# A residual adapter with layer norm: block turns read contiguously, and another plan of who does what

## Chip, cores and metric

One core of a Trainium2 chip runs the whole program. The metric is device time in microseconds of one launch; lower is better.

## The reference, cut to what matters

x holds 128 batches of 128 rows and 512 columns, in fp32. Each batch b has a language number, which picks its W1 (512×128), b1, W2 (128×512), b2, gamma and beta out of ten.

```python
h = relu(einsum('bsh,bha->bsa', x, W1[ids]) + b1[ids][:, None, :])
adapted = einsum('bsa,bah->bsh', h, W2[ids]) + b2[ids][:, None, :]
y = x + adapted
normed = (y - mean(y)) * rsqrt(var(y) + 1e-5)          # along the 512 columns
out = x + normed * gamma[ids][:, None, :] + beta[ids][:, None, :]
```

## The kernel before, in words

One batch is one tile: 128 rows on the partitions, 512 columns. x is loaded four batches at a time (`load_x`, L80) and stored two at a time (`store`, L464). W2 and the spread rows of b2, gamma and beta stay in SBUF, as does W1 of all ten languages once it is loaded (from batch 17 on).

The path of a batch b, engine by engine:

- TensorE transposes the four 128-column blocks of x into PSUM (`transpose_x`, L317), ScalarE copies them to SBUF (`copy_xT`, L325). ScalarE copies the batch's W1 into its own tile (`stage_w1`, L311), since the language number is known at run time only. TensorE multiplies W1 by the transposed x, four accumulated products into PSUM (`down`, L342); ScalarE adds b1 and applies relu (`relu`, L352); TensorE multiplies by W2 into one of five PSUM buffers (`up`, L356).
- GpSimd adds x and b2 beforehand (`add_b2`, L329, into one of four buffers) and x and beta into the output tile (`add_beta`, L335). VectorE adds the former to the product, with the sum of each row as a by-product (`residual`, L380); ScalarE takes the sum of squares (`square`, L403) and, for two batches at once, the mean and the first guess of the reciprocal root; VectorE refines that in three small steps (`rstd`), then applies mean and gamma (`scale`, L448) and the reciprocal deviation and beta (`finish`, L457). `finish` frees the PSUM buffer and completes the output.

Three letters vary the path, in patterns of 16 batches:

- `KINDS`, between batch `MIDDLE` and batch 128 - `LAST`: an "E" batch is *seeded*. ScalarE copies x into the PSUM buffer first (`seed`, L307), the product accumulates onto it, and VectorE's `residual` adds b2 by the register of the batch's language. GpSimd then adds only beta. A "P" batch has x + b2 from GpSimd. Outside, the kind is "-": there GpSimd adds b2 too, or, for a few batches, VectorE in an instruction of its own (`vector_b2`, L375).
- `TURNS`, from batch `TURNED` on: a "T" batch goes as above. A "w" batch has its W1 loaded from HBM by a DMA of SyncE (`load_late`, L572) instead of ScalarE's copy. An "F" batch is *turned*: its W1 is loaded from HBM (`load_first`, L169), its x is loaded a second time, block by block, so that 32×32 blocks lie where they belong (`load_blocks`, L284, four DMAs of 64 KB), and VectorE transposes all of these blocks in one instruction (`turn_blocks`, L291). Neither TensorE's transposes nor ScalarE's copy are needed for it.

W1 tiles and the second copies of x share seven buffers (`wp`).

The order of the work is written out by a plan. Each step is entered with a due time in units of batches (`at`, `at_pair`, L641 to L694); the steps are issued in the order of these times, and `keep` (L57) holds each engine to that order. `BATCH` has the times of the steps of one batch relative to its number, `PAIR` those of two batches 2g and 2g+1 relative to 2g + 3; `EDGE` takes the place of `PAIR` where one of the pair's kinds is "-". The engines wait for each other by semaphores alone. `lid` (L151) loads four language numbers into an engine's registers; it stands in that engine's queue like any other step. Batches 123 to 127 and the end are written out by hand (L699 to L849).

Of the kernel before, what the change touches and what calls it, by code (L numbers as in the profile page):

```python
# [8 lines left out]
FP = mybir.dt.float32  # L9
# [4 lines left out]
ET = mybir.EngineType  # L14
PSUM = bass.MemoryType.PSUM

P = 128
G = 4
# [2 lines left out]
EARLY = 17  # L21
LATE = 17
U = 2
MIDDLE = 27
TURNED = 31
LAST = 8
KINDS = 'EPPPPPEPEEPPEPPP'
TURNS = 'TTTTFTTTTTwwFTTw'
SEEDED = 'E'
ON_GPSIMD = 'P'  # L30
BATCH = dict(turn=-0.49, copy=0.12, r=0.1, beta=-0.56, relu=1.24, w1=-0.83, up=2.11, load=-5.63, r_late=-0.51)
SEED = {'E': 1.88}
PAIR = dict(stat=0.23, square=0.35, means=1.55, root=1.82, scale0=2.66, n1=2.4, n2=3.195, n3=3.37, scale1=3.4, end0=3.66, end1=4.28)
EDGE = dict(stat=0.59, square=0.73, means=1.74, root=2.0, scale0=3.04, n1=2.83, n2=3.375, n3=3.69, scale1=4.03, end0=4.06, end1=4.58)


@with_exitstack
def cond_resid_kernel(ctx: ExitStack, tc: tile.TileContext, x, itok, W1, b1, W2, b2, gamma, beta, out):
# [8 lines left out]
    nc = tc.nc  # L47
    B, S, H = x.shape
    L, _, A = W1.shape
    KC = H // P  # L50
# [6 lines left out]
    def keep(ins):  # L57

        engine = ins.ins.engine
        if engine in last:  # L60
            tc.add_manual_dep(ins.ins, last[engine], behind, reason="kept order")
        last[engine] = ins.ins.name
        return ins
# [6 lines left out]
    wp = ctx.enter_context(tc.tile_pool(name="wp", bufs=7))  # L70
# [7 lines left out]
    E = B - 5  # L78
# [11 lines left out]
    rows = rp.tile([P, H], FP, tag="r", name="rows")  # L90
    b1r = const.tile([L, A], FP, name="b1r")
    w1 = const.tile([P, L, KC, A], FP, name="w1")
# [49 lines left out]
    lids, w1s = {}, {}  # L142
# [8 lines left out]
    def lid(b, engine):  # L151
        g = b // G
        if (g, engine) not in lids:
            loads, vals = nc.values_load_multi_w_load_instructions(
                lang[0:1, g * G : (g + 1) * G],
                engines=[engine],
                min_val=0,
                max_val=L - 1,
                skip_runtime_bounds_check_because="clamped on the chip to 0..L-1 above",
            )  # L160
            for ins in loads:
                keep(ins)
            lids[g, engine] = vals
        return lids[g, engine][b % G]
# [102 lines left out]
    def kind(b):  # L267
        return KINDS[b % len(KINDS)] if MIDDLE <= b < B - LAST else "-"

    def turn(b):  # L270
        return TURNS[b % len(TURNS)] if TURNED <= b < B - LAST - 2 else "-"

    def seeded(b):
        return kind(b) in SEEDED
# [7 lines left out]
    x2s = {}  # L282

    def load_blocks(b):  # L284
        x2s[b] = wp.tile([P, H], FP, tag="w1s", name=f"x2_{b}")
        for i in range(KC):
            src = x[b, :, i * P : (i + 1) * P].rearrange("(j c) e -> c j e", c=32)
            dst = x2s[b][32 * i : 32 * (i + 1), :].rearrange("c (j e) -> c j e", j=4)
            keep(nc.sync.dma_start(out=dst, in_=src))

    def turn_blocks(b):  # L291
        xT[b] = tp.tile([P, H], FP, tag="xT", name=f"xT_{b}")
        src = x2s.pop(b).rearrange("p (j r k) -> p j k r", j=4, k=KC)
        dst = xT[b].rearrange("p (j k c) -> p j k c", j=4, k=KC)
        keep(nc.vector.transpose(dst, src))

# [170 lines left out]
    def on(b):  # L467
        return 0 <= b < B
# [172 lines left out]
    def at(when, step, *args):  # L641
        plan.append((when, len(plan), step, args))

    for b in range(B):
        if b >= 20 and b % G == 0:
            at((11 if b == 20 else b - 7) - 0.01, load_x, b // G)
        if b >= 3:
            for n, engine in ((b + 5, ET.Activation), (b + 5, ET.PE), (b + 2, ET.DVE), (b + 6, ET.Pool)):
                if on(n):
                    at(b + 0.99, lid, n, engine)  # L650
        if turn(b) in "Fw":
            at(b + BATCH["load"] - 1, lid, b, ET.SP)
            at(b + BATCH["load"], load_first if turn(b) == "F" else load_late, b)
        if turn(b) == "F":
            at(b + BATCH["load"], load_blocks, b)
            at(b + BATCH["turn"], turn_blocks, b)
        elif 5 <= b <= E - 2:
            at(b, transpose_x, b)
            at(b + BATCH["copy"], copy_xT, b)
        if 4 <= b <= E - 3:  # L660
            add_to = b + (BATCH["r"] if seeded(b) else BATCH["r_late"])
            at(add_to, add_b2, b)
            at(b + BATCH["beta"], add_beta, b)
            at(b + 1.1, down, b)
            at(b + BATCH["relu"], relu, b)
        if seeded(b):
            at(b + SEED[kind(b)], seed, b)
        if FIRST <= b <= E - 1 and turn(b) not in "Fw":
            at(b + BATCH["w1"], stage_w1, b)
        if 2 <= b <= E - 4:  # L670
            at(b + BATCH["up"], up, b)

    begun = [(step, n) for n in (E - 7, E - 6, E - 5) for step in (vector_b2, residual, square)]
    begun += [(scalar_means, E // 2 - 3), (deviation, E // 2 - 3), (scale, E - 7), (rstd, E // 2 - 3, 1)]
# [1 line left out]
    def at_pair(g, when, step, *args):  # L676
        if g < E // 2 - 3 or (step, *args) in begun:
            at(2 * g + 3 + when, step, *args)

    for g in range(E // 2 - 1):  # L680
        b = 2 * g
        when = EDGE if "-" in (kind(b), kind(b + 2)) else PAIR
        for j in (0, 1):
            at_pair(g, j + when["stat"] - 0.01, vector_b2, b + j)
            at_pair(g, j + when["stat"], residual, b + j)
            at_pair(g, j + when["square"], square, b + j)
        at_pair(g, when["means"], scalar_means, g)
        at_pair(g, when["root"], deviation, g)
        for n in (1, 2, 3):
            at_pair(g, when[f"n{n}"], rstd, g, n)  # L690
        for j in (0, 1):
            at_pair(g, when[f"scale{j}"], scale, b + j)
            at_pair(g, when[f"end{j}"], finish, b + j)
        at_pair(g, when["end1"] + 0.001, store, g)  # L694
# [192 lines left out]
```

## Time and profile before

| | |
|---|---|
| median of 3 runs | 303.43 us (302.5 to 304.01) |
| profiled execution | 303.28 us, its span 301.5 us |
| granted TensorE clock, mean | 0.996 |
| moved by DMA | 88.1 MB, 292 GB/s on average |

The profile is of one execution. A row of a group gives the line, the engine, the operation, the tiles that it writes and reads, the count, the busy time, and the mean duration of one in ns. PE is TensorE, PEld its weight loads, DVE VectorE, ACT ScalarE, POOL GpSimd, SP SyncE. An instruction of an engine usually begins some 0.1 us before the one ahead of it is recorded as ended, so a step from start to start is shorter than a duration. A row of the waits says who waited for whom, for how long in all, how often, and the longest.

### The profile page before, as it was taken

To read this page: it belongs to the slowest core of one execution; us is meant where nothing else is said; L and a number is where in the kernel's file an instruction comes from. 1 tells how busy PE (TensorE), PEld (TensorE's weight loads), DVE (VectorE), ACT (ScalarE), POOL (GpSimd) and SP (SyncE) were. 2 spreads that over 40 slices of the span, in tenths; PEclk is the share of its full clock that TensorE was granted. 3 is DMA by queue.
4 is the path that set the end of the run, shared out by engine and by line. 5 is a ranking of instruction groups with operands and counts; after the bars stand their busy time and mean duration, and the time that the engine had idled before them with its cause. 6 is when DMAs were issued, how large, how long until landed. Compare 5 with 4: busy or idle time off the path is not lost.

```text
span 301.5 us, 7148 instructions
## 1 busy us (share of the span) xinstructions
PE 294.0 (98%) x1783; PEld 216.9 (72%) x1783; DVE 291.9 (97%) x775; ACT 273.1 (91%) x760; POOL 272.8 (90%) x229
## 2 busy tenths in 40 slices
PE   7999999999999999999999999999999999999993
PEld 3858787767777777777777777777677777777761
DVE  5999999999999999999999999999999999999995
ACT  4978789889999989999999989999999999999883
POOL 1199998999999999999999999999998999989852
PEclk9999999999999999999999999999999999999998
DMA  6999999987869899799997999699997899884625
GB/s 227 390 388 365 346 331 400 405 307 227 318 237 315 245 365 282 252 312 321 315 299 241 305 312 308 253 314 293 330 292 229 269 296 363 287 279 150 224 79 215
DMA packets 61724, 88.10 MB, mean 292 GB/s; under 512 B 3274, under 2 KB 24277, under 8 KB 61683
## 3 DMA queue, kind: packets, MB, share of 16 engines
q1 hardware_dynamic: 61622, 87.59, 86.7%
q8 instruction: 15, 0.25, 0.3%
q14 instruction: 27, 0.21, 0.2%
q10 hardware_dynamic: 60, 0.05, 0.1%
HBM read 54.07 MB, written 33.55 MB: 291 GB/s over the span
## 4 chain that ended last, share of the span: by engine, by line
PE 55%; DVE 21%; issue 11%; DMA 6%; ACT 4%; DVEq 1%; SPq 1%; POOL 0%; ACTq 0%; POOLq 0%
PE ph L346 21%; PE py L368 18%; PE pxT L323 10%; DVE py L452 6%; DVE py L386 6%; PE py L360 5%; DVE o L461 5%; DMA w<-in_L_cond_W_dram 3%; DMA out_dram<-o 2%; ACT sq L409 1%; DMA w1s<-in_L_cond_W_dram 1%; DVE o L546 1%; ACT xT L327 1%; DVE py L378 1%; DVE part L425 1%
## 5 line engine op out<-in xcount | busy, mean ns | idle before, releaser
L340 POOL TENSOR_TENSOR o<-x,beta_b 128x512 f32<-128x512 f32 x121 | 153.3, 1282 | 14.0 <-DVE beta_b L258 12.7
L346 PE MATMUL ph<-xT,w1s 128*128 128x128 f32 x1024 | 135.4, 275 | 0.0
L346 PEld LDWEIGHTS ph<-xT,w1s 128*128 128x128 f32 x1024 | 125.7, 192 | 6.9 <-ACT hT L354 5.7
L333 POOL TENSOR_TENSOR r<-x,b_b 128x512 f32<-128x512 f32 x85 | 108.8, 1280 | 3.6 <-DVE rstd L428 3.6
L368 PE MATMUL py<-w,hT 128*128 x200 | 104.0, 601 | 0.9 <-DVE o L461 0.6
L323 PEld LDWEIGHTS pxT<-ident,x 128*128 128x128 f32 x468 | 60.9, 150 | 59.9 <-issue 39.3
L452 DVE SCALAR_TENSOR_TENSOR py<-py,nmean,gamma_b 128x512 f32<-128x512 f32 x124 | 92.8, 749 | 1.7 <-issue 1.7
L409 ACT ACTIVATE sq<-py,sum 128x512 f32<-128x512 f32 x124 | 85.8, 692 | 7.9 <-DVE rstd L428 5.8
L461 DVE SCALAR_TENSOR_TENSOR o<-py,rstd,o 128x512 f32<-128x512 f32 x116 | 85.5, 747 | 0.0
L327 ACT COPY xT<-pxT 128x512 f32<-128x512 f32 x117 | 68.5, 585 | 5.5 <-PE pxT L323 4.7
L323 PE MATMUL pxT<-ident,x 128*128 128x128 f32 x468 | 71.9, 277 | 0.0
L386 DVE SCALAR_TENSOR_TENSOR py<-py,r 128x512 f32<-128x512 f32 x90 | 62.2, 691 | 0.0
L354 ACT ACTIVATE hT<-ph,b1T 128x128 f32<-128x128 f32 x128 | 47.7, 373 | 5.9 <-PE ph L346 4.3
L314 ACT COPY w1s<-w 128x512 f32 x81 | 50.4, 622 | 0.0
L368 PEld LDWEIGHTS py<-w,hT 128*128 128x128 f32 x200 | 30.4, 191 | 4.9 <-DVE o L461 3.4
L360 PE MATMUL py<-w,hT 128*128 x56 | 29.3, 604 | 0.0
L409 ACT ACTIVATION_READ_ACCUMULATOR sq<-py,sum 128x1 f32 x124 | 25.8, 208 | 0.0
L386 DVE SCALAR_TENSOR_TENSOR py<-py,b_b 128x512 f32<-128x512 f32 x28 | 19.4, 692 | 0.4 <-PE py L360 0.2
L309 ACT COPY py<-x 128x512 f32<-128x512 f32 x28 | 16.7, 596 | 0.0
L419 ACT ACTIVATE root<-ssq,eps 128x2 f32<-128x2 f32 x62 | 16.5, 265 | 0.0
L400 ACT ACTIVATE nmean<-sum 128x2 f32<-128x2 f32 x61 | 12.9, 212 | 0.0
L386 DVE DVE_READ_ACCUMULATOR py<-py,r 128x1 f32 x90 | 12.6, 140 | 0.0
(79 smaller groups left out, 147.2 us busy)
## 6 DMA issues: line engine op xcount, KB each, us to landing
out_dram<-o SPq DMA_DIRECT2D x62, 512.0 KB, 5.0
x<-in_x_dram SPq DMA_DIRECT2D x27, 1024.0 KB, 7.2
w1s<-in_L_cond_W_dram SPq DMA_DIRECT2D x47, 256.0 KB, 6.3
x<-in_x_dram SPq DMA_DIRECT2D x10, 512.0 KB, 6.1
x<-in_x_dram SPq DMA_DIRECT2D x44, 64.0 KB, 4.0
w<-in_L_cond_W_dram SPq DMA_DIRECT2D x4, 640.0 KB, 8.2
w<-in_L_cond_W_dram SPq DMA_DIRECT2D x1, 1792.0 KB, 9.9
w<-in_L_cond_W_dram SPq DMA_DIRECT2D x1, 768.0 KB, 5.4
```

What stands on the lines that cost most here:

```text
L314: keep(nc.scalar.copy(w1s[b].rearrange("p k a -> p (k a)"), src))
L323: keep(nc.tensor.transpose(pxs[b][:, k, :], cols, ident))
L327: keep(nc.scalar.copy(xT[b], pxs.pop(b)))
L333: keep(nc.gpsimd.tensor_tensor(rs[b], xb(b), b2_b[:, bass.ds(v * H, H)], ALU.add))
L340: keep(nc.gpsimd.tensor_tensor(os[g][:, j, :], xb(b), beta_b[:, bass.ds(v * H, H)], ALU.add))
L346: nc.tensor.matmul(phs[b], lhsT=w1s[b][:, k, :], rhs=xT_of(b, k), start=(k == 0), stop=(k == KC - 1))
L354: keep(nc.scalar.activation(hT[b], phs.pop(b), AF.Relu, bias=b1T[:, bass.ds(lid(b, ET.Activation), 1)]))
L368: keep(nc.tensor.matmul(ys[b], lhsT=hT[b], rhs=w2[:, bass.ds(v * H, H)], start=not m, stop=True))
L386: nc.vector.scalar_tensor_tensor(ys[b], ys[b], 1.0, r, ALU.mult, ALU.add, accum_out=sum_of(b))
L409: nc.scalar.activation(sq, ys[b], AF.Square, bias=col(sums, b), scale=-float(H), accum_out=col(ssqs, b))
L452: nc.vector.scalar_tensor_tensor(ys[b], ys[b], col(nmeans, b), gamma_b[:, bass.ds(v * H, H)], ALU.add, ALU.mult)
L461: nc.vector.scalar_tensor_tensor(o, ys[b], rstds[g][:, j : j + 1], o, ALU.mult, ALU.add)
```

## The change

- `turn_blocks` reads its source so that the 32 columns of a block are neighbours. Before, they were four elements apart, and the columns of the transposed x were interleaved accordingly. The rows of W1 must be in the same order, so turned batches load W1 with the new `load_rows`: four DMAs of 32 partitions, each partition holding four rows that are 32 apart.
- `KINDS` has four E among 16 letters instead of five (place 9 is now P), between batches 26 and 123 instead of 27 and 119. `TURNS` has one w (place 9) instead of three (places 10, 11, 15); the two F, places 4 and 12, stay. Turned or late batches begin at 32 instead of 31 and end at 121 instead of 117.
- Batches of kind "-" take their steps' times from the new `BATCH_EDGE`, and all tables of times have new values.
- VectorE's `lid` is entered behind a `finish`, for the four batches that follow; before, it was entered at the end of the step of every fourth batch, for the batches from two further on.

```diff
-MIDDLE = 27
-TURNED = 31
-LAST = 8
-KINDS = 'EPPPPPEPEEPPEPPP'
-TURNS = 'TTTTFTTTTTwwFTTw'
+MIDDLE = 26
+TURNED = 32
+LAST = 4
+KINDS = 'EPPPPPEPEPPPEPPP'
+TURNS = 'TTTTFTTTTwTTFTTT'
-BATCH = dict(turn=-0.49, copy=0.12, r=0.1, beta=-0.56, relu=1.24, w1=-0.83, up=2.11, load=-5.63, r_late=-0.51)
-SEED = {'E': 1.88}
-PAIR = dict(stat=0.23, square=0.35, means=1.55, root=1.82, scale0=2.66, n1=2.4, n2=3.195, n3=3.37, scale1=3.4, end0=3.66, end1=4.28)
-EDGE = dict(stat=0.59, square=0.73, means=1.74, root=2.0, scale0=3.04, n1=2.83, n2=3.375, n3=3.69, scale1=4.03, end0=4.06, end1=4.58)
+BATCH = dict(turn=0.19, copy=0.16, r=-0.36, beta=-0.13, relu=1.26, w1=-0.77, up=2.66, load=-5.59, r_late=0.22)
+BATCH_EDGE = dict(copy=0.2, r=0.05, r_late=1.05, beta=1.06, relu=1.3, w1=-0.6, up=2.5)
+SEED = {'E': 1.69}
+PAIR = dict(stat=0.22, square=0.34, means=1.98, root=1.9, scale0=3.03, n1=2.43, n2=3.115, n3=3.28, scale1=3.4, end0=3.67, end1=4.32)
+EDGE = dict(stat=0.6, square=0.68, means=1.75, root=1.77, scale0=2.64, n1=2.65, n2=3.592, n3=3.62, scale1=3.64, end0=3.66, end1=4.66)
...
+    def load_rows(b):
+        w1s[b] = wp.tile([P, KC, A], FP, tag="w1s", name=f"w1s_{b}")
+        rows = W1[bass.ds(lid(b, ET.SP), 1)].rearrange("o (i k r) a -> i (o r) k a", i=4, k=KC)
+        for i in range(4):
+            keep(nc.sync.dma_start(out=w1s[b][32 * i : 32 * (i + 1)], in_=rows[i]))
+
     def turn_blocks(b):
         xT[b] = tp.tile([P, H], FP, tag="xT", name=f"xT_{b}")
-        src = x2s.pop(b).rearrange("p (j r k) -> p j k r", j=4, k=KC)
+        src = x2s.pop(b).rearrange("p (j k r) -> p j k r", j=4, k=KC)
         dst = xT[b].rearrange("p (j k c) -> p j k c", j=4, k=KC)
         keep(nc.vector.transpose(dst, src))
...
     for b in range(B):
+        when = BATCH_EDGE if kind(b) == "-" else BATCH
...
-            for n, engine in ((b + 5, ET.Activation), (b + 5, ET.PE), (b + 2, ET.DVE), (b + 6, ET.Pool)):
+            for n, engine in ((b + 5, ET.Activation), (b + 5, ET.PE), (b + 6, ET.Pool)):
...
-            at(b + BATCH["load"], load_first if turn(b) == "F" else load_late, b)
+            at(b + BATCH["load"], load_rows if turn(b) == "F" else load_late, b)
...
+        if b % G == 0 and on(b + G):
+            at_pair(g, when["end0"] + 0.001, lid, b + G, ET.DVE)
```

In the loop over the batches, the times of `copy_xT`, `add_b2`, `add_beta`, `relu`, `stage_w1` and `up` are read from `when` instead of `BATCH`. Counted over the program, ScalarE has 91 copies of W1 instead of 81 and 24 seeds instead of 28; GpSimd has 94 additions of b2 instead of 90; SyncE issues 44 + 17 + 9 loads of single W1 instead of 28 + 19; TensorE's instructions are the same ones.

More of the change, by code (lines that the diff above doesn't have):

```diff
@@ L658, in cond_resid_kernel @@
             at(b, transpose_x, b)
-            at(b + BATCH["copy"], copy_xT, b)
+            at(b + when["copy"], copy_xT, b)
         if 4 <= b <= E - 3:
-            add_to = b + (BATCH["r"] if seeded(b) else BATCH["r_late"])
-            at(add_to, add_b2, b)
-            at(b + BATCH["beta"], add_beta, b)
+            at(b + (when["r"] if seeded(b) else when["r_late"]), add_b2, b)
+            at(b + when["beta"], add_beta, b)
             at(b + 1.1, down, b)
-            at(b + BATCH["relu"], relu, b)
+            at(b + when["relu"], relu, b)
         if seeded(b):
@@ L668, in cond_resid_kernel @@
         if FIRST <= b <= E - 1 and turn(b) not in "Fw":
-            at(b + BATCH["w1"], stage_w1, b)
+            at(b + when["w1"], stage_w1, b)
         if 2 <= b <= E - 4:
-            at(b + BATCH["up"], up, b)
+            at(b + when["up"], up, b)
     begun = [(step, n) for n in (E - 7, E - 6, E - 5) for step in (vector_b2, residual, square)]
```

## The prediction

> **What bounds the kernel now.** I read the page first, for the load of each engine.
>
> ```profile
> span 301.5 us, 7148 instructions
> PE 294.0 (98%) x1783; PEld 216.9 (72%) x1783; DVE 291.9 (97%) x775; ACT 273.1 (91%) x760; POOL 272.8 (90%) x229
> PE 55%; DVE 21%; issue 11%; DMA 6%; ACT 4%; DVEq 1%; SPq 1%; POOL 0%; ACTq 0%; POOLq 0%
> ```
>
> Four engines are loaded to 90% or more, and the chain that ended last (third line) changes hands between TensorE and VectorE. Which of them sets the pace? The table of windows answers that for the middle, from the first weights of batch 36 to those of batch 116: 80 batches, that is five rounds of the 16-letter patterns, with ten block turns, 25 seeds and 15 late W1 loads.
>
> ```profile
> core 0: us, PE busy (x) PEld busy (x) DVE busy (x) ACT busy (x) POOL busy (x), PEclk, DMA share, GB/s
> 91.93:266.28 174.35, 173.91 (x1083) 130.29 (x1081) 174.00 (x451) 166.22 (x471) 170.72 (x140) 1.00 0.90 295
> 94.37:105.32 10.95, 10.95 (x72) 8.32 (x71) 10.92 (x30) 10.84 (x33) 10.95 (x10) 1.00 0.91 284
> ```
>
> VectorE is idle for 0.35 of 174.35 us: it is full. GpSimd is idle for 3.63, ScalarE for 8.13. TensorE looks full too, but its ends are modelled, so I go by its starts. TensorE's timeline, the rows of the down products only:
>
> ```profile
> 55.77 1.16 PE L346 MATMUL ph<-xT,w1s 128*128 128x128 f32 x8
> 58.38 1.06 PE L346 MATMUL ph<-xT,w1s 128*128 128x128 f32 x8
> 60.58 1.06 PE L346 MATMUL ph<-xT,w1s 128*128 128x128 f32 x8
> 63.23 1.06 PE L346 MATMUL ph<-xT,w1s 128*128 128x128 f32 x8
> 65.42 1.06 PE L346 MATMUL ph<-xT,w1s 128*128 128x128 f32 x8
> 68.04 1.06 PE L346 MATMUL ph<-xT,w1s 128*128 128x128 f32 x8
> ...
> 87.98 1.06 PE L346 MATMUL ph<-xT,w1s 128*128 128x128 f32 x8
> 89.74 1.05 PE L346 MATMUL ph<-xT,w1s 128*128 128x128 f32 x8
> 91.93 1.06 PE L346 MATMUL ph<-xT,w1s 128*128 128x128 f32 x8
> 94.37 1.06 PE L346 MATMUL ph<-xT,w1s 128*128 128x128 f32 x8
> ...
> 266.28 1.06 PE L346 MATMUL ph<-xT,w1s 128*128 128x128 f32 x8
> ```
>
> Undisturbed, a batch takes 2.19 us (89.74 to 91.93, or 63.23 to 65.42), and 1.76 where the next batch is turned by VectorE and its four TensorE transposes are left out (87.98 to 89.74). Right after a turn comes a stall: 91.93 to 94.37 is 2.44. By starts, TensorE needs 70 × 2.19 + 10 × 1.76 = 170.9 us for the middle and takes 174.35: **3.5 us of stall** in ten turns. Batches 21, 23 and 25 (the first six rows) stall by 0.42, 0.46 and 0.43: **1.3 us** more. The eleventh turn lies behind the window; at the mean of the ten it adds 0.35. So some **5.2 us** of TensorE's time is waiting, and no more can be won here without less work on TensorE. The table of waits says for what:
>
> ```profile
> PEld py L368 <- DVE o L461: 3.4, 14, 0.4
> DVE py L452 <- issue: 1.7, 4, 0.7
> POOL r L333 <- DVE rstd L428: 3.6, 3, 1.4
> POOL o L340 <- DMA out_dram<-o: 1.3, 1, 1.3
> POOL r L485 <- DVE py L386: 1.1, 1, 1.1
> ```
>
> An up product waits for a PSUM buffer that `finish` (L461) frees: TensorE stands because VectorE is late. VectorE's own idle time (second row) is four waits with no releaser, at a `scale` behind a load of batch numbers into registers (`lid`).
>
> **The change part by part.** *The turns.* Eleven before and eleven after (places 4 and 12, batches 36 to 116). Each reads with a step of 16 bytes now and contiguously then. The groups:
>
> ```profile
> L295 DVE STREAM_TRANSPOSE xT<-x 128x512 f32<-128x512 f32 x11 | 12.4, 1125 | 0.0
> L258 DVE STREAM_SHUFFLE beta_b<-four 128x512 f32<-128x512 f32 x10 | 6.6, 752 | 0.0
> L378 DVE TENSOR_TENSOR py<-py,b_b 128x512 f32<-128x512 f32 x6 | 4.2, 694 | 0.2 <-PE py L368 0.2
> ```
>
> The trace has no contiguous turn. Its bounds: 1125 ns, if the step costs nothing, and 694, the cheapest 512-column row here; reading fewer lines can't make it slower. I take 752, the shuffle, which also moves whole 512-column rows between partitions and reads contiguously: 373 ns less each, **4.1 us** in eleven (between 0 and 4.7). In the middle VectorE's load falls from 174.0 to 170.3, which is TensorE's 170.9: the pace passes to TensorE.
>
> A rule speaks against this gain: "VectorE: DVE Perf Modes" of the Trainium skill, section "The three transpose paths", gives 311 ns for a VectorE transpose of 128×128 in bf16. Four times that, an estimate, is 1244, which would make 1125 the normal price of 512 columns, and by it this term of the sum is nothing (rival A). "SBUF — State Buffer" of the Trainium skill, section "Door 1: The DMA port swizzle", speaks for the gain: SBUF is read in lines of 16 bytes and each new line costs, so a step of 16 bytes pays at every element. No run here shows yet which of the two holds.
>
> *The turn's place.* It moves behind `scale` of batch b-6 and a small step. Before, the turn of 36 ran from 89.09 and its product began at 91.93 on TensorE:
>
> ```profile
> 89.09 1.12 DVE L295 STREAM_TRANSPOSE xT<-x 128x512 f32<-128x512 f32 x1
> 90.12 0.72 DVE L452 SCALAR_TENSOR_TENSOR py<-py,nmean,gamma_b 128x512 f32<-128x512 f32 x1
> 90.75 0.16 DVE L425 SCALAR_TENSOR_TENSOR part<-part,root 128x2 f32<-128x2 f32 x1
> 90.82 0.70 DVE L386 SCALAR_TENSOR_TENSOR py<-py,r 128x512 f32<-128x512 f32 x1
> ```
>
> It ended at 90.21, 1.72 us early. The two steps take 0.70 (90.12 to 90.82) and the quicker turn gives 0.37 back, so 1.39 us of cover is left: nothing. Without the cover, TensorE would wait at each product of a turned batch.
>
> *W1 of these batches* now comes in four DMAs of 64 KB instead of one of 256 KB, in the same pieces and shape as the block loads of x:
>
> ```profile
> w1s<-in_L_cond_W_dram SPq DMA_DIRECT2D x47, 256.0 KB, 6.3
> x<-in_x_dram SPq DMA_DIRECT2D x44, 64.0 KB, 4.0
> L289 SPq DMA_DIRECT2D x<-in_x_dram x44: 312/430/1242, 76.8 to 255.0; - x44
> ```
>
> Three more issues of 0.43 us are 1.3 us on SyncE per turn; behind them queue the block loads of x, then stores and later loads. The loads start 5.6 batches ahead, 12 us at 2.19; eight issues and a landing are 8 × 0.43 + 4.0 = 7.4. Hidden. Ten late W1 loads fewer (16 to 6) take 2.6 MB of 88 off the queues.
>
> *Late loads and seeds.* Those ten W1 are copied by ScalarE again, and four seeds fewer are copied (24 for 28):
>
> ```profile
> 92.68 0.58 ACT L327 COPY xT<-pxT 128x512 f32<-128x512 f32 x1
> 93.16 0.62 ACT L314 COPY w1s<-w 128x512 f32 x1
> 93.67 0.37 ACT L354 ACTIVATE hT<-ph,b1T 128x128 f32<-128x128 f32 x1
> ```
>
> ```profile
> L309 ACT COPY py<-x 128x512 f32<-128x512 f32 x28 | 16.7, 596 | 0.0
> ```
>
> Such a copy holds the queue for 0.51 us (93.16 to 93.67), the seed, 26 ns shorter, about as long: 10 × 0.51 - 4 × 0.51 = 3.1 us more, in the middle 10 - 5 copies, 166.2 to 168.8. That fits under 170.9, barely.
>
> *GpSimd* gets the b2 addition of the batches no longer seeded (place 9, five batches; batch 120 becomes seeded): 94 for 90. An addition takes 170.72 / 140 = 1.22 us: **4.9 us more on an engine that has little left**. In the middle alone it needs 170.7 + 5 × 1.22 = 176.8, so it must live on its lead. How large is that? Before the sum for batch 123 it waited 4.9 us because it was ahead (3.6 + 1.3 in the table of waits), and that sum (GpSimd's timeline, then VectorE's) lay ready for a while:
>
> ```profile
> 280.83 1.28 POOL L485 TENSOR_TENSOR r<-x,b_b 128x512 f32<-128x512 f32 x1
> ```
>
> ```profile
> 286.15 0.69 DVE L386 SCALAR_TENSOR_TENSOR py<-py,r 128x512 f32<-128x512 f32 x1
> ```
>
> It ended at 282.11 and was used at 286.15: 4.04. So 4.9 + 4.0 - 4.9 = **4.0 us** is all that the rest may come earlier before GpSimd is late. The 1.3 in it, the wait for a store, should go: up to batch 25 the b2 addition now stands before the beta addition, so GpSimd reaches that beta one addition later.
>
> *Batches up to 25.* VectorE's two `finish` of a pair stood next to each other; now a residual, a `scale` and a small step lie between, so buffers come free evenly, and `lid` stands behind a `finish`, which covers it, instead of before a `scale`. I take the three stalls, 1.3 us, as gone (between 0 and 1.7, VectorE's four waits). The tail's pairs take the step times of the middle; its hand-written end is the same: nothing.
>
> *The sum.* VectorE could give 4.1 + 1.7 = 5.8, TensorE 5.2, GpSimd 4.0. The least counts: 4.0. As three engines then lie within 2% of each other in the middle (170.9, 170.3, 168.8) and the fourth has no spare, I take 0.5 off for waits that pass between them, about what VectorE, the bound, lost in the middle (0.35). The profiled execution took 303.28 us (its span of 301.5 and 1.8 around it): 303.28 - 3.5 = 299.8, and against the median of the runs, 0.15 higher, **299.9 us**.
>
> **The rivals.** *A: the turn is no quicker* (its time is the transposition's, not the step's; the change then does not do what it says). For: the trace shows no contiguous turn. Against: 1125 stands far above every other 512-column row. VectorE stays full in the middle, and only the early 1.3 is won: 303.28 - 1.3 = 302.0.
>
> *B: GpSimd binds harder.* The wait for the store stays (its landing is the queue's matter, not GpSimd's): 2.7 is then its allowance, less 0.5: 303.28 - 2.2 = 301.1.
>
> *C: slower, by ScalarE.* Its load would be 168.8 in a middle of 170.9, so 2.1 us of its 8.1 us of waiting may stay. If all of it stays, the middle takes 168.8 + 8.1 = 176.9, 2.6 more than before, and over the 98 batches of the patterns 3.2: 306.5; it turns slower from 5.5 us on. For: relu and square each wait for another engine. Against: in batches 37 to 41, with three seeds in five (second row of the windows), ScalarE was busy for 10.84 of 10.95 and TensorE kept 2.19 all the same.
>
> **How the numbers follow.** The forecast 0.58, A 0.17, B 0.13, C 0.12. The forecast's own range is 298.4 to 301.2. The range of 8 in 10 takes in B and A: 298.2 to 303.2; C is left out. A measurement of this kernel can tell 0.5%, 1.5 us. Faster by more (under 301.9): the forecast, most of B and a third of A, 0.72; within: the rest of A and B and a mild C, 0.18; slower: 0.10.
>
> **What would show it.** The turn's group near 750 ns instead of 1125; TensorE's step after a turn near 2.19 instead of 2.44; starts 2.19 apart from batch 20 to 26; GpSimd without its three waits for VectorE and, late, VectorE's residual waiting for GpSimd; ScalarE's waits in the middle near 2 us. A turn over 1.0 us, or new waits of TensorE for ScalarE, would make it wrong.

## The result, and the profile after

The changed kernel takes 300.69 us (median of ten runs, 300.02 to 301.93); the kernel before takes 303.69 beside it. The ratio is 0.9904, with an interval of 0.9881 to 0.9927: about 1% faster. One of the ten runs of the kernel before took 508.05 us; the ratio is of the others. The profiled execution took 301.23 us with a span of 298.8, where the one before had 303.28 and 301.5.

The head of the page, the load of each engine, and the shares of the chain that ended last, for the changed kernel:

```profile
span 298.8 us, 7251 instructions
PE 290.7 (97%) x1783; PEld 214.7 (72%) x1783; DVE 288.9 (97%) x775; ACT 277.2 (93%) x766; POOL 277.4 (93%) x233
PE 81%; DVE 6%; ACT 4%; DMA 3%; issue 3%; SPq 1%; DVEq 0%; POOL 0%; ACTq 0%; POOLq 0%
```

VectorE's share of the last chain fell from 21% to 6% and TensorE's rose from 55% to 81%: the pace has passed to TensorE. But TensorE still waits, and the groups and the windows show where. First the groups of the turn and of ScalarE's copies of W1 and of seeds:

```profile
L302 DVE STREAM_TRANSPOSE xT<-x 128x512 f32<-128x512 f32 x11 | 7.7, 703 | 0.0
L321 ACT COPY w1s<-w 128x512 f32 x91 | 56.7, 623 | 0.0
L316 ACT COPY py<-x 128x512 f32<-128x512 f32 x24 | 14.4, 599 | 0.0
```

A turn takes 703 ns instead of 1125. Now the windows of the changed kernel, with the columns of the prediction's table (span, then busy time of PE, PEld, DVE, ACT, POOL). The first row is the middle, batches 36 to 116; the second is the stretch from batch 36 to batch 44, the third that from 44 to 52, so both run from a turned batch to the next:

```profile
90.91:264.02 173.11, 173.11 (x1083) 129.35 (x1081) 171.00 (x451) 170.12 (x476) 173.11 (x141) 1.00 0.87 282
90.91:107.99 17.08, 17.08 (x110) 12.89 (x109) 16.98 (x46) 16.74 (x48) 17.08 (x14) 1.00 0.84 263
107.99:125.50 17.51, 17.51 (x111) 12.97 (x110) 17.24 (x46) 17.31 (x50) 17.51 (x16) 1.00 0.90 300
```

The middle takes 173.11 us, 1.24 less than before, but 2.2 more than the 170.9 that TensorE needs. The first stretch is exactly TensorE's need (7 × 2.19 + 1.75 = 17.08; 1.75 is the step ahead of a turned batch). The second is 0.43 longer, and ScalarE is busy in it for 17.31 us, more than TensorE's 17.08. The four later stretches of the second kind take 17.69, 17.50, 17.49 and 17.50, those of the first kind 17.08 or 17.09: the 2.2 us lie in the second kind alone. TensorE's timeline, the rows of the down products only, shows the places:

```profile
58.18 1.06 PE L353 MATMUL ph<-xT,w1s 128*128 128x128 f32 x8
...
69.15 1.06 PE L353 MATMUL ph<-xT,w1s 128*128 128x128 f32 x8
...
90.91 1.06 PE L353 MATMUL ph<-xT,w1s 128*128 128x128 f32 x8
93.10 1.06 PE L353 MATMUL ph<-xT,w1s 128*128 128x128 f32 x8
...
112.39 1.06 PE L353 MATMUL ph<-xT,w1s 128*128 128x128 f32 x8
114.64 1.16 PE L353 MATMUL ph<-xT,w1s 128*128 128x128 f32 x8
116.93 1.06 PE L353 MATMUL ph<-xT,w1s 128*128 128x128 f32 x8
119.12 1.06 PE L353 MATMUL ph<-xT,w1s 128*128 128x128 f32 x8
121.47 1.06 PE L353 MATMUL ph<-xT,w1s 128*128 128x128 f32 x8
```

The first two rows are batches 21 and 26: five steps in 10.97 us, 2.19 each; the early stalls are gone. Behind the turned batch 36 the step is 2.19 as well (90.91 to 93.10; before 2.44). But from batch 46 (112.39) on come steps of 2.25, 2.29, 2.19 and 2.35: stalls that were not there before. ScalarE's timeline at that place:

```profile
112.11 0.71 ACT L416 ACTIVATE sq<-py,sum 128x512 f32<-128x512 f32 x1
112.68 0.23 ACT L416 ACTIVATION_READ_ACCUMULATOR sq<-py,sum 128x1 f32 x1
112.94 0.27 ACT L426 ACTIVATE root<-ssq,eps 128x2 f32<-128x2 f32 x1
113.14 0.19 ACT L407 ACTIVATE nmean<-sum 128x2 f32<-128x2 f32 x1
113.23 0.56 ACT L334 COPY xT<-pxT 128x512 f32<-128x512 f32 x1
113.70 0.62 ACT L321 COPY w1s<-w 128x512 f32 x1
114.22 0.37 ACT L361 ACTIVATE hT<-ph,b1T 128x128 f32<-128x128 f32 x1
```

One instruction follows the other without a wait, and so it goes on to 117.98. TensorE's transposes wait there for ScalarE's copy of the transposes before (0.8 us in three waits between 112 and 121.5). In the middle as a whole, the row of this wait in the changed kernel, then in the kernel before:

```profile
PEld pxT L330 <- ACT xT L334: 8.3, 32, 0.4
PEld pxT L323 <- ACT xT L327: 7.2, 30, 0.2
```

The sum is not the point, since a weight load often waits while a product still runs; new is the longest one, 0.37 us, which stands behind the product of batch 46 and at the same place of every later round. The longest of the steps, 2.35, has another cause, a wait too short for the table: the up product of the seeded batch 48 waits for its seed. ScalarE's row of that seed:

```profile
119.42 0.60 ACT L316 COPY py<-x 128x512 f32<-128x512 f32 x1
```

It ends at 120.02, and the product's weights begin to load at 120.07. In all five rounds of the middle the seed comes that late at this place. Five rows of the table of waits, whole execution:

```profile
PEld pxT L330 <- ACT xT L334: 13.3, 48, 0.7
PEld ph L353 <- ACT hT L361: 7.0, 13, 0.6
DVE py L393 <- PE py L367: 1.4, 7, 0.3
POOL o L347 <- DMA out_dram<-o: 1.3, 1, 1.3
ACT sq L416 <- DVE rstd L435: 0.2, 1, 0.2
```

TensorE's wait for a PSUM buffer that `finish` frees (3.4 us before) is gone, and so is GpSimd's for VectorE (3.6). ScalarE's square waits 0.2 us for VectorE, before 5.8. VectorE itself now waits for products of TensorE (third row). Two of the rows go against the prediction: in the middle ScalarE has lost nearly all of its waiting (the 0.2 us of the last row, where the kernel before waited for 6.6), and GpSimd's wait for a store has stayed at 1.3.

### The profile page after: what moved, and what is told of

Same layout as the page of the kernel before. It is cut to its first block, busy times and chain, and to the rows that moved or that the text cites. A ratio compares the mean times of both kernels' runs of the same rounds, so it can differ in the third digit from the quotient of the medians.

```text
span 298.8 us, 7251 instructions
## 1 busy us (share of the span) xinstructions
PE 290.7 (97%) x1783; PEld 214.7 (72%) x1783; DVE 288.9 (97%) x775; ACT 277.2 (93%) x766; POOL 277.4 (93%) x233
## 4 chain that ended last, share of the span: by engine, by line
PE 81%; DVE 6%; ACT 4%; DMA 3%; issue 3%; SPq 1%; DVEq 0%; POOL 0%; ACTq 0%; POOLq 0%
PE ph L353 33%; PE py L375 26%; PE pxT L330 15%; PE py L367 7%; DMA w<-in_L_cond_W_dram 3%; DVE py L393 2%; ACT sq L416 1%; DVE o L553 1%; DVE py L459 1%; ACT w1s L321 1%; ACT xT L334 1%; SPq L173 1%; DVE n L559 0%; ACT hT L361 0%; ACT root L426 0%
## 5 line engine op out<-in xcount | busy, mean ns | idle before, releaser
L347 POOL TENSOR_TENSOR o<-x,beta_b 128x512 f32<-128x512 f32 x121 | 155.8, 1306 | 12.9 <-DVE beta_b L259 11.6
L340 POOL TENSOR_TENSOR r<-x,b_b 128x512 f32<-128x512 f32 x89 | 116.1, 1305 | 0.0
L468 DVE SCALAR_TENSOR_TENSOR o<-py,rstd,o 128x512 f32<-128x512 f32 x116 | 86.8, 748 | 0.0
L393 DVE SCALAR_TENSOR_TENSOR py<-py,r 128x512 f32<-128x512 f32 x94 | 64.9, 690 | 1.4
L321 ACT COPY w1s<-w 128x512 f32 x91 | 56.7, 623 | 0.0
L375 PEld LDWEIGHTS py<-w,hT 128*128 128x128 f32 x208 | 31.7, 192 | 2.1 <-DMA w<-in_L_cond_W_dram 1.2
L393 DVE SCALAR_TENSOR_TENSOR py<-py,b_b 128x512 f32<-128x512 f32 x24 | 16.6, 693 | 1.5 <-PE py L367 1.4
L316 ACT COPY py<-x 128x512 f32<-128x512 f32 x24 | 14.4, 599 | 0.0
L407 ACT ACTIVATE nmean<-sum 128x2 f32<-128x2 f32 x61 | 11.7, 192 | 0.0
```

Of the source, the lines that this page charges most:

```text
L321: keep(nc.scalar.copy(w1s[b].rearrange("p k a -> p (k a)"), src))
L340: keep(nc.gpsimd.tensor_tensor(rs[b], xb(b), b2_b[:, bass.ds(v * H, H)], ALU.add))
L347: keep(nc.gpsimd.tensor_tensor(os[g][:, j, :], xb(b), beta_b[:, bass.ds(v * H, H)], ALU.add))
L375: keep(nc.tensor.matmul(ys[b], lhsT=hT[b], rhs=w2[:, bass.ds(v * H, H)], start=not m, stop=True))
L393: nc.vector.scalar_tensor_tensor(ys[b], ys[b], 1.0, r, ALU.mult, ALU.add, accum_out=sum_of(b))
L468: nc.vector.scalar_tensor_tensor(o, ys[b], rstds[g][:, j : j + 1], o, ALU.mult, ALU.add)
```

## Experiments

**Theory S**, as the expectations call it: the new letters, not the turn or the new times, hold the change back. ScalarE's load is uneven, and the stretch behind place 12, with seven copies of W1 and two seeds, is longer on ScalarE than on TensorE. **Its rivals**: GpSimd, with one more b2 addition in 16 batches, sets the pace as the prediction had it; or the new order of the steps does. The time behind "against" is that of the kernel before, on the same chip and in the same set of runs. There were three such sets (303.91, 303.52 and 303.74 us before), so kernels of different sets are compared by their ratios.

### strided: the new plan without the new turn

The changed kernel with the old read, and W1 of turned batches in one DMA again.

```diff
-        src = x2s.pop(b).rearrange("p (j k r) -> p j k r", j=4, k=KC)
+        src = x2s.pop(b).rearrange("p (j r k) -> p j k r", j=4, k=KC)
...
-            at(b + BATCH["load"], load_rows if turn(b) == "F" else load_late, b)
+            at(b + BATCH["load"], load_first if turn(b) == "F" else load_late, b)
```

> The changed kernel with its turns back on the old reading (step of four elements, W1 in one DMA), all else as changed. If the reading alone made the turn quicker, the turn takes 1125 ns again, VectorE is full again in the middle (some 174 us for 80 batches), and of the 2.9 us won at most the early 1.3 stays: about 302.4 us, TensorE stalling by 0.25 or more after each turn. If the plan brought the gain, about 300.7 as the changed kernel.

Measured: 304.32 us against 303.91, ratio 1.0015 [0.9996, 1.0034]. The turn's group and the middle of this kernel:

```profile
L302 DVE STREAM_TRANSPOSE xT<-x 128x512 f32<-128x512 f32 x11 | 12.6, 1145 | 0.0
```

```profile
90.84:267.37 176.53, 176.35 (x1083) 130.40 (x1081) 175.15 (x451) 169.79 (x476) 176.53 (x144) 1.00 0.84 276
```

The turn costs 1145 ns again. The middle is 2.2 us longer than before (174.35), though the batches up to 36 are 1.3 faster here as in the changed kernel. The expected 302.4 us was 1.9 too low: the plan by itself gains nothing, since what it wins early it loses in the middle. All of the change's gain hangs on the turn.

### contig: the new turn without the new plan

The kernel before with the contiguous read and `load_rows` alone.

```diff
-        src = x2s.pop(b).rearrange("p (j r k) -> p j k r", j=4, k=KC)
+        src = x2s.pop(b).rearrange("p (j k r) -> p j k r", j=4, k=KC)
...
-            at(b + BATCH["load"], load_first if turn(b) == "F" else load_late, b)
+            at(b + BATCH["load"], load_rows if turn(b) == "F" else load_late, b)
```

> The kernel before with the contiguous turn and its row-ordered W1 alone, with its own patterns and times. Theory S (ScalarE paces the changed kernel's middle, because of the ten W1 copies added): here ScalarE keeps its relief, the stalls after the turns go and nothing takes their place: the middle takes 171.2 instead of 174.35, and with the early stalls left the time is about 300.2, no worse than the changed kernel. Theory G (GpSimd paces it, with 28 additions per round): here it has 27, 33.3 us per round, so also about 300.2. If neither, and TensorE and VectorE hold each other up, about 301.5.

Measured: 299.68 us against 303.91, ratio 0.985 [0.9825, 0.9876]: faster than the whole change. Its turns take 704 ns, and its middle:

```profile
91.42:262.78 171.36, 171.24 (x1082) 129.10 (x1081) 170.73 (x452) 167.13 (x472) 171.36 (x140) 1.00 0.92 291
```

That is 0.5 over TensorE's 170.9, with ScalarE at 167.13 instead of 170.12. The early stalls are still there (2.33 to 2.44 at batches 21, 25, 27 and 30). Both of the new plan's effects can be read from the two kernels: 1.75 us lost in the middle, and about half a microsecond won up to batch 36 (4 to 36 takes 70.94 us here and 70.43 in the changed kernel).

### late15: one copy of W1 less behind place 12

The changed kernel, with place 15 late again as before.

```diff
-TURNS = 'TTTTFTTTTwTTFTTT'
+TURNS = 'TTTTFTTTTwTTFTTw'
```

> The changed kernel with one more late W1 load per round (place 15), which takes five copies in the middle off ScalarE and nothing off GpSimd. Theory S: the stalls of 0.4 us per round go, middle 171.2 instead of 173.1, time about 298.7. Theory G: the rounds stay at 34.6 us, time about 300.7.

Measured: 300.03 us against 303.91, ratio 0.9867 [0.984, 0.9894]. The same two stretches as above, batches 36 to 44 and 44 to 52:

```profile
90.71:107.80 17.09, 17.09 (x110) 12.90 (x109) 16.98 (x46) 16.76 (x48) 17.09 (x15) 1.00 0.88 278
107.80:124.94 17.14, 17.14 (x110) 12.85 (x109) 16.85 (x45) 16.64 (x48) 17.14 (x15) 1.00 0.92 309
```

One copy taken out brings ScalarE from 17.31 to 16.64 in the second stretch and the stretch from 17.51 to 17.14. That is S's cause at S's place, and batch 48's product no longer waits for its seed. The whole middle, however, took 172.49 us, not 171, and by the ratios the time can't be told from the changed kernel's: two stalls of 0.5 and 0.7 remain, in its second and third round. The rows of VectorE ahead of the first, then of ScalarE, then the register load that stands between VectorE's two rows in its queue:

```profile
137.21 0.75 DVE L468 SCALAR_TENSOR_TENSOR o<-py,rstd,o 128x512 f32<-128x512 f32 x1
138.47 0.70 DVE L393 SCALAR_TENSOR_TENSOR py<-py,b_b 128x512 f32<-128x512 f32 x1 [0.51 <-PE pxT L330]
```

```profile
141.98 0.69 ACT L416 ACTIVATE sq<-py,sum 128x512 f32<-128x512 f32 x1 [0.56 <-DVE rstd L435]
```

```profile
L155 DVEq TENSOR_LOAD <-lang x1: 1591/1591/1591, 136.7 to 136.7; - x1
```

The load of the language numbers (`lid`), now behind a `finish`, took 1.59 us here and ended at 138.3; the `finish` that covers it ended at 137.96. The releaser named in the row (TensorE's transposes) had long been done. At the second stall the load took 1.73 us. VectorE runs on without a gap and doesn't make up for it; ScalarE's square waits for it 3.5 us later, and behind that TensorE stalls.

### five: five seeds again, in the new plan

```diff
-KINDS = 'EPPPPPEPEPPPEPPP'
+KINDS = 'EPPPPPEPEEPPEPPP'
```

> The changed kernel with five seeded batches per round again (place 9): five more seed copies in the middle for ScalarE (0.51 us each), one addition less per round for GpSimd. Theory S: the rounds grow by up to 0.5 us, time 302.5 to 303. Theory G: GpSimd needs 33.3 us per round and the middle falls to 171.2, time about 298.8.

Measured: 303.44 us against 303.91, ratio 0.9974 [0.996, 0.9989]. Its middle, and a row of its waits near the end (274 to 284):

```profile
90.87:264.65 173.78, 173.78 (x1082) 129.17 (x1081) 171.70 (x451) 171.87 (x481) 171.57 (x140) 1.00 0.88 281
```

```profile
ACT py L316 <- DVE o L553: 1.4, 1, 1.4
```

GpSimd has room again (busy for 171.57 of 173.78), and the middle is slower than the changed kernel's all the same: taking work off GpSimd and giving it to ScalarE costs 0.7. That speaks against the rival GpSimd. The total time says less: with the pattern ending at 124, batch 121 becomes seeded, its copy waits for a buffer in ScalarE's queue, and 1.9 us are lost at batch 122, outside the middle.

### patterns: the old letters with the new times

The changed kernel with `TURNED`, `LAST`, `KINDS` and `TURNS` of before.

```diff
-TURNED = 32
-LAST = 4
-KINDS = 'EPPPPPEPEPPPEPPP'
-TURNS = 'TTTTFTTTTwTTFTTT'
+TURNED = 31
+LAST = 8
+KINDS = 'EPPPPPEPEEPPEPPP'
+TURNS = 'TTTTFTTTTTwwFTTw'
```

> The changed kernel with the letters of the kernel before (three late W1 loads and five seeds per round, LAST 8, TURNED 31); the contiguous turn, the new times, the new early order and MIDDLE 26 stay. Theory S (ScalarE paced the changed kernel's middle): its middle falls from 173.1 to some 171.4, as with the turn alone, and the early stalls stay away: about 299.0. If the new times themselves cost the 1.7 us, the middle stays at 173 and the time at 300.7.

Measured: 299.12 us against 303.52, ratio 0.9842 [0.9817, 0.9866]. Its middle:

```profile
90.66:262.24 171.58, 171.58 (x1083) 129.06 (x1082) 170.60 (x452) 168.37 (x472) 170.91 (x140) 1.00 0.92 291
```

With the old letters the new times cost the middle next to nothing (171.58, where contig has 171.36). So the rival that the new order alone holds the change back falls, and the new letters are needed for the loss. That they make it without the new times is not shown: no kernel has both new patterns with the old times.

### contig_kinds and contig_turns: each new pattern alone

Both are contig with one more line:

```diff
-KINDS = 'EPPPPPEPEEPPEPPP'
+KINDS = 'EPPPPPEPEPPPEPPP'
```

> The kernel before with the contiguous turn and the new KINDS (four seeds; GpSimd gets five more b2 additions, ScalarE loses four or five copies). Theory S alone: ScalarE has more room, nothing else matters, 299.7 or a little less. The prediction's term for GpSimd: with the turn alone its sum for batch 123 lay ready 2.7 us early; five additions of 1.23 us more make it 3.5 us late, so VectorE waits for GpSimd near the end and the time is about 302.5 to 303.

```diff
-TURNS = 'TTTTFTTTTTwwFTTw'
+TURNS = 'TTTTFTTTTwTTFTTT'
```

> The kernel before with the contiguous turn and the new TURNS (one late W1 load per round instead of three; ScalarE copies ten W1 more). Theory S: ScalarE's load in the middle goes from 167.1 to some 172.2, more than TensorE's 171.4, and the middle to about 173.8: 302 us. If ScalarE was not the limit: 299.7, or less, since 2.6 MB fewer are loaded.

Measured: contig_kinds 301.42 us against 303.52, ratio 0.9937 [0.9917, 0.9958]; contig_turns 301.49, ratio 0.9926 [0.9904, 0.9949]. Each is slower than contig, by 1.7 to 1.8 us in the medians and by 2.3 to 2.6 by the ratios, for different reasons. The middle of contig_kinds, then of contig_turns:

```profile
92.04:262.92 170.88, 170.88 (x1083) 129.17 (x1082) 170.33 (x451) 165.12 (x467) 170.88 (x140) 1.00 0.92 293
```

```profile
91.77:265.39 173.62, 172.77 (x1083) 129.54 (x1081) 170.34 (x450) 170.41 (x481) 171.18 (x140) 1.00 0.88 281
```

With four seeds and the old late loads the middle is TensorE's need to a hundredth. But GpSimd pays: three of its additions, from its timeline, and VectorE's residuals and TensorE near the end of the same kernel:

```profile
99.74 1.30 POOL L339 TENSOR_TENSOR r<-x,b_b 128x512 f32<-128x512 f32 x1
100.98 2.52 POOL L346 TENSOR_TENSOR o<-x,beta_b 128x512 f32<-128x512 f32 x2
103.44 1.28 POOL L339 TENSOR_TENSOR r<-x,b_b 128x512 f32<-128x512 f32 x1
```

```profile
282.25 0.70 DVE L392 SCALAR_TENSOR_TENSOR py<-py,r 128x512 f32<-128x512 f32 x1 [1.33 <-POOL r L491]
...
284.70 0.70 DVE L392 SCALAR_TENSOR_TENSOR py<-py,r 128x512 f32<-128x512 f32 x1 [0.69 <-POOL r L491]
```

```profile
286.97 1.16 PE L352 MATMUL ph<-xT,w1s 128*128 128x128 f32 x8 [1.97 <-ACT hT L360]
```

Three additions take 103.44 - 99.74 = 3.70, or 1.233 each. With four seeds a round of 16 batches has 16 + 12 of them: 34.5 us, where TensorE needs 34.18. So GpSimd falls back 0.3 us in each round. Its b2 sums were ready 1.7 us early at batch 36 and 0.0 at batch 116, and at the end VectorE waits for two of them, 2.0 us together. The prediction's limit is real, in this mix.

contig_turns lacks no time on GpSimd. Its ScalarE is busy for 170.41, with 18 copies of W1 and seeds in a round instead of 16, nine in each of the two stretches. The step ahead of the turn at place 12 takes 2.14 us instead of 1.75 in all five rounds, so the stretch with three seeds is 0.4 to 0.9 longer; the other, with two seeds and seven copies as in the changed kernel, keeps TensorE's 17.09. A row of the waits says what the long step waits for:

```profile
PEld py L366 <- ACT py L315: 1.7, 6, 0.3
```

Five of the six are in the middle, one in each round: the up product of the seeded batch at place 9 waits 0.31 us for ScalarE's seed. So the engine is S's, but the count of copies in a stretch doesn't tell the whole: nine copies behind place 12 cost nothing here. It is the late seed that stops TensorE, and where it stands in ScalarE's queue counts too.

### contig_lid: the register load behind a finish

contig, with VectorE's `lid` where the change puts it; the order of the early batches stays as before.

```diff
-            for n, engine in ((b + 5, ET.Activation), (b + 5, ET.PE), (b + 2, ET.DVE), (b + 6, ET.Pool)):
+            for n, engine in ((b + 5, ET.Activation), (b + 5, ET.PE), (b + 6, ET.Pool)):
...
+        if b % G == 0 and on(b + G):
+            at_pair(g, when["end0"] + 0.001, lid, b + G, ET.DVE)
```

> The kernel before with the contiguous turn, and VectorE's loads of batch numbers placed behind finish as in the changed kernel, but with the old early order. If these loads make the early stalls, the 0.8 us that the turn alone still loses between batches 20 and 31 go: about 298.9. If the pairwise finish makes them, they stay: about 299.7.

Measured: 298.65 us against 303.52, ratio 0.9836 [0.981, 0.9861]. All of the starts from batch 16 to 34 are 2.19 apart: the early stalls came from `lid`, and the new spacing of the two `finish` wasn't needed for them. The other kernels bear this out: the six with `lid` at its old place all stall between batches 20 and 30, the seven with the new place never do. One row of its waits shows what is left, waits with no releaser at residuals behind a long load:

```profile
DVE py L392 <- issue: 1.8, 4, 0.5
```

They make the middle 171.95 us, 0.6 longer than contig's, and by the ratios the two kernels can't be told apart. The early stalls are gone, but a long load now stalls at another place.

### step8: a step of 8 bytes instead of 16

contig, with the turn reading every second column and W1's rows to match, so that two of the elements that it reads lie in each 16 bytes.

```diff
-        src = x2s.pop(b).rearrange("p (j r k) -> p j k r", j=4, k=KC)
-        dst = xT[b].rearrange("p (j k c) -> p j k c", j=4, k=KC)
+        src = x2s.pop(b).rearrange("p (g r k) -> p g k r", g=8, k=2)
+        dst = xT[b].rearrange("p (g k c) -> p g k c", g=8, k=2)
```

> The turn alone on the kernel before (as contig), but read with a step of two elements, 8 bytes, and W1's rows ordered to match. If a read costs by the 16-byte lines that it opens, two reads share a line and the turn takes what the contiguous one takes, 704 ns. If the cost goes with the step, it lies between 704 and 1125, near 850 to 900. The time of the program: 299.7 in the first case, about 300.5 in the second.

Measured: 299.72 us against 303.74, ratio 0.9862 [0.9844, 0.9879]. The group of its turn:

```profile
L301 DVE STREAM_TRANSPOSE xT<-x 128x512 f32<-128x512 f32 x11 | 7.7, 704 | 0.0
```

A step of 8 bytes costs nothing: 704 ns, as when contiguous. Only the step of 16 costs, 421 ns in 1125. So the source needn't be contiguous: two elements in each 16 bytes are enough. That fits a price per 16 bytes opened; a limit on the step itself, between 8 and 16 bytes, would give the same three numbers, and no run tells the two apart.

### one_w1: are the three added DMAs hidden?

contig, with W1 of turned batches loaded by `load_first` in one DMA. It leaves out the new order of W1's rows, so it computes another product for these batches.

```diff
-            at(b + BATCH["load"], load_rows if turn(b) == "F" else load_late, b)
+            at(b + BATCH["load"], load_first if turn(b) == "F" else load_late, b)
```

> The turn alone on the kernel before (as contig), but the turned batches' W1 comes in one DMA in the old row order, so the product of these batches is another one. If the four DMAs of 64 KB in 512-byte pieces are hidden, as the prediction had it: the time of contig, 299.7, within 0.3. If they cost SyncE or the queues something that reaches the end: up to 1 us less.

Measured: 299.88 us against 303.74, ratio 0.9867 [0.985, 0.9884]; contig has 0.985 [0.9825, 0.9876]. No difference beyond the noise, and in neither kernel's waits does TensorE wait for the W1 of a turned batch: hidden, as predicted.

### best: what the runs point to

contig_lid, and for batches of kind "-" GpSimd's two additions in the order of the change, so that the b2 sums aren't late behind the quicker start.

```diff
-MIDDLE = 27
+MIDDLE = 26
...
+BATCH_EDGE = dict(r_late=1.05, beta=1.06)
...
-            add_to = b + (BATCH["r"] if seeded(b) else BATCH["r_late"])
+            edge = BATCH_EDGE if kind(b) == "-" else BATCH
+            add_to = b + (BATCH["r"] if seeded(b) else edge["r_late"])
             at(add_to, add_b2, b)
-            at(b + BATCH["beta"], add_beta, b)
+            at(b + edge["beta"], add_beta, b)
```

> contig_lid with GpSimd's order of the changed kernel for the batches up to 25 (the b2 addition ahead of the beta addition, patterns from batch 26). GpSimd's lead was 0.3 us at batch 27 and nothing at 37 in contig_lid; one addition earlier, it should be 1.2 us or more, and VectorE should not wait for GpSimd there. TensorE was at its floor already: 298.4 to 298.7.

Measured: 298.45 us against 303.74, ratio 0.9828 [0.981, 0.9847]. It is the fastest median of all, though contig, contig_lid and patterns can't be told from it. Against the changed kernel's ratio of 0.9904 [0.9881, 0.9927] the intervals lie apart.

## Why the prediction was right, and where it was wrong

The forecast was 299.9 us and the measurement 300.69: the direction and most of the size were right, and the one term that caps the gain was put on the wrong engine. Between the two spans 2.7 us were won: 1.28 up to batch 36, 1.24 in the middle and 0.43 behind it, less 0.26 ahead of batch 4.

- *The turn* was right as a mechanism and a little small: 752 ns taken, 703 measured, 4.6 us of VectorE's time instead of 4.1. The nearest row by kind, the shuffle, was worse here than the cheapest 512-column row (694), which the prediction had as its bound. Rival A falls. Its price of 302.0 was too low besides: strided, the plan without the quicker turn, takes 304.32. The estimate of 1244 for 512 columns from the 311 ns that the Trainium skill gives ("VectorE: DVE Perf Modes", "The three transpose paths") doesn't hold for this form. The rule of 16-byte lines of the Trainium skill ("SBUF — State Buffer", "Door 1: The DMA port swizzle"), by which two hits in a line are enough, agrees with 1125, 704 and 703 ns at steps of 16, 8 and 4 bytes.
- *VectorE's 4.1 us and, in the middle, TensorE's 3.5 of 5.2* were right as what could be given and won: contig_kinds reaches 170.88 in the middle, where the prediction had 170.9. Behind turns the step is 2.19, as forecast.
- *The step that failed* is the one on late loads and seeds: "That fits under 170.9, barely." The sum of 168.8 was for the whole middle, in which ScalarE measured 170.12, and it hid how the copies lie. Counted by stretch, the one behind place 12 has nine copies of W1 and seeds, the other eight, at 0.51 each. In the longer one ScalarE was busy for 17.31 us where TensorE needs 17.08, and the time left in the other didn't help it: its copies and the seed at place 0 came late for TensorE. That left 2.2 of the middle's 3.5 us unwon. The reason given against rival C, that ScalarE kept up with 10.84 of 10.95 busy, was five batches long, and two late W1 loads followed them (places 10 and 11); that ScalarE only lived on a lead there is likely, but not shown. Rival C's mechanism thus came, in a mild form, and with it a sign by which the prediction said that it would be wrong, new waits of TensorE for ScalarE.
- *GpSimd* was taken for the limit, at 4.0 us less 0.5, and by luck of size the wrong limit gave nearly the right sum (3.5 forecast, 2.7 between the two spans). In the changed kernel VectorE never waits for it: the rows of the b2 sums for batches 123 and 124, then of the residual of 123, show a sum that ends at about 281.9 and is used at 283.62.

```profile
280.61 2.54 POOL L492 TENSOR_TENSOR r<-x,b_b 128x512 f32<-128x512 f32 x2
```

```profile
283.62 0.69 DVE L393 SCALAR_TENSOR_TENSOR py<-py,r 128x512 f32<-128x512 f32 x1
```

  The lead of 4.0 has shrunk to 1.7, about as the working has it, and from batch 26 on no b2 sum has less than 1.6. GpSimd is busy without a gap in the middle (173.11 of 173.11), but its lead doesn't fall there: 2.1 us at batch 36, 2.6 at batch 116. Once ScalarE is relieved (contig_kinds) the limit does bind, and only there. Rival B had its premise, the wait for the store, come true, and its 301.1 us lies nearer to the measurement than the forecast; but GpSimd was not what bound, so that is luck too.
- *The early batches*: 1.3 us forecast, 1.28 measured (batch 4 to 36 in 70.43 us for 71.71). The three stalls went, as forecast. That the sum fits so well is partly luck: a fourth stall that the prediction left out (0.23 at batch 30) went too, and new ones of 0.3 together came at batches 32, 34 and 36. The prediction gave two causes; contig_lid shows that moving `lid` is enough.
- *The wait for a store* should have gone and stayed at 1.3. It cost nothing, since GpSimd was ahead by more.
- *W1 in four DMAs* was right in its result and wrong in a number: the 64 KB pieces landed in 6.7 us in contig and 3.2 in the changed kernel, not in 4.0. The cover of 12 us was enough for both: neither shows TensorE waiting for the W1 of a turned batch.

What stays open: the letters were tried in these combinations only. By the copies of W1 and seeds in 16 batches, the middle's mean round is 34.17 us with 15 (contig_kinds), 34.27 and 34.31 with 16 (contig, patterns), 34.62 with 17 (the changed kernel), 34.72 and 34.76 with 18 (contig_turns, five). That order fits S. The other kernels with 16 and the quicker turn lie between 34.31 and 34.50; late15, with the 34.50, has the two stalls behind long register loads. In the changed kernel, contig_turns and five a seeded product waits for its seed in every round; in contig, patterns and contig_kinds none does. But why contig_turns pays for 18 copies in one of its stretches and five in both (17.41 and 17.34) isn't settled, nor what keeps a stretch from using the time that ScalarE has left in the one before: the order of the copies, or the few buffers between ScalarE and TensorE. No run changed either by itself.

## What to carry to other kernels

Where several engines are full to within 2%, compare their loads stretch by stretch, between the points where the order repeats, and not only over the whole: here the longest stretch decided, and what ScalarE had left elsewhere didn't help it. A change that takes work off one engine by giving it to others should be run in its parts; here one part, the turn, alone beat the whole change, and another gave part of the gain back. And look at the step with which an instruction reads: 8 bytes cost this transpose nothing, 16 bytes cost 421 ns in 1125.

## What the runs showed of the hardware

The load of language numbers from SBUF into VectorE's registers varies more than any instruction that it stands among. All of its loads in late15 from 20 us on, least, median and most in ns:

```profile
L155 DVEq TENSOR_LOAD <-lang x29: 342/637/1734, 23.9 to 266.5; - x29
```

The arithmetic instructions beside it vary by at most 34 ns, form by form (666 to 700 ns for a residual). In the other kernels the longest load takes between 0.96 us (strided) and 1.80 (one_w1). It stands in the engine's queue, where an instruction of 0.75 us covers the median and not the longest. The page doesn't count it as busy, so its stall is put down to "issue" or to some engine that was long done.
